# Block transposes of softmax weights through DMA: pieces of 4 KB instead of 1 KB, and twelve of sixteen DMAs on the sync engine

## The chip, the cores and the metric

The kernel runs on one core of a Trainium2 chip. A core has five engines that run their own instruction streams: TensorE (PE, with its weight loads listed apart as PEld), VectorE (DVE), ScalarE (ACT), GpSimd (POOL) and SyncE (SP). They meet through semaphores. DMAs are issued by an engine (here SP or POOL) into a queue and carried by 16 DMA engines. The metric is the device time of one execution in microseconds (us), the median over runs.

## The reference

Four transformer blocks act one after the other on x (4 batches, 1024 tokens, 256 channels), with a short context of 77 tokens for the cross-attention layers. All is float32. The change touches block L1, which has three attention layers with 4 heads of 64 channels: layer 0 attends to the context, layers 1 and 2 attend to the tokens themselves. Cut to what matters:

```python
def _mha_layer(q, k, v, Wq, bq, Wk, bk, Wv, bv, gamma, beta):
    Q = jax.nn.relu(q @ Wq + bq)          # likewise K, V; split into 4 heads of 64
    scores = jnp.einsum('hbqd,hbkd->hbqk', Qh, Kh) / jnp.sqrt(jnp.float32(dh))
    scores = jnp.where(key_mask[None, :, None, :] == 0.0, NEG, scores)
    attn = jax.nn.softmax(scores, axis=-1) * query_mask[None, :, :, None]
    out = jnp.einsum('hbqk,hbkd->hbqd', attn, Vh)
    return _layer_norm(out + q, gamma, beta)

q, k, v = (queries, keys, values)
for i in range(3):
    enc = _mha_layer(q, k, v, Wq[i], ...)
    enc = jax.nn.leaky_relu(enc @ Wff[i] + bff[i], negative_slope=0.2) + enc
    q, k, v = (enc, enc, enc)
```

## The kernel before

The program is laid out by a Python planner. Each (layer, batch) is an item. While an item attends, step by step ("units"), the planner weaves in the preparation of the next item (transposing x, projecting Q, K and V) and the end of the previous one (norm and feed-forward); each woven step has a cost, and `Pump` takes as many as the unit's share asks for. `Pipe.later(kind, delay, f)` puts off work to a later unit. The order on PE is the order in which the program is written. The order on the other engines is chosen by the compiler's scheduler, which also inserts all semaphores, and a buffer tag has a fixed number of slots that are reused in turn. DMAs issued by SP use eight completion semaphores in turn, those issued by POOL eight others.

A self layer of L1 (`Self4`) goes, per batch, over 2 pairs of heads p and 8 tiles t of 128 query tokens. One unit is one (p, t):

- `scores`: eight matmuls (L1262) give the scores of two heads, 128 queries by 1024 keys each, in two PSUM tiles `ss`. DVE takes the maximum of each row (L1273), ACT writes exp(score - max) into the SBUF tile `PR` and the row sums beside it (L1279).
- `turned_by_blocks`, one unit later: the weights must be transposed, since the next matmul contracts over the keys. DVE transposes every 32x32 block in place (L1291). For that to be enough on the DVE side, ACT has written the keys in the order (c, k, i) rather than (k, c, i), where a key's number is 128 k + 32 c + i. After every second tile t, sixteen DMAs (L1298) carry the blocks to the partitions where they belong: the DMA (c, a) reads partitions 32a to 32a+31 of `PR` and writes partitions 32c to 32c+31 of `PT`. It moves 128 KB: on each of 32 partitions four pieces (2 tiles by 2 heads) of 256 numbers, 1 KB each. a = 0 and 2 are issued by SP, a = 1 and 3 by POOL. Two tiles t, with their sixteen DMAs, are called a pair; there are 64 pairs in layers 1 and 2.
- `weighted`: two units and three units after the pair's second transposes are issued, 16 matmuls each (L1334) multiply V by `PT`, then ACT copies the sums (L1512) and, after four tiles, `normal` divides by the row sums and adds to x.

`PR` (tag "E") and `PT` (tag "B") have two slots of 16 KB per partition each. So the exp of a pair waits for the sixteen DMAs of the pair two before it, and the DMAs of a pair wait for the L1334 matmuls of the pair two before it.

Other users of the two DMA-issuing engines in this stage: SP loads the weights of the next layer (L1028, L1033), moves the mask row `nrow` (L1179), which the matmul L1231 reads, and `thirds` (a bias row cut into three bfloat16 rows by DVE, L2060 to L2063, each moved by a small DMA, L2061), which L1187 and L1402 read. POOL computes powers for the norms (L1385, between DVE's L1383 and L1387).

The flag `net.blocks` is true in the branch that runs here, taken when the mask leaves only a few keys to attend to in the network's first self-attention; the other branch (`turned`) transposes on PE and does not run.

Of the kernel before, what the change touches and what calls it, by code (L numbers as in the profile page):

```python
# [17 lines left out]
P = 128  # L18
NB, S, C, SC = 4, 1024, 256, 77
NT = S // P  # L20
# [102 lines left out]
class Pipe:  # L123
# [15 lines left out]
    def unit(self, scores=None, cost=0.0):  # L139
        self.call("full")  # L140
        if scores:
            scores()
        self.call("next")
        self.now += cost
        self.pump()
        for kind in ("turn", "late", "col"):
            self.call(kind)
        self.u += 1

    def run(self, items):  # L150
        pump = Pump(self, 1, items[0].start(), [])
        pump.until(lambda: items[0].halves >= 1)
        left = pump.lists[0]
        before = None
        for a, b in zip(items, items[1:]):
            b.prev = a
        for i, item in enumerate(items):
            last = i + 1 == len(items)
            first = left + ([] if last else items[i + 1].start())
            second = (before.end() if before else []) + (item.end() if last else [])  # L160
            left = []
            idle = item.idle()
            self.pump = pump = Pump(self, item.units + idle, item.more() + first, second)
            for _ in range(idle):
                self.unit()
            for scores in item.attend():
                self.unit(scores, item.cost)
            assert last or not any(pump.lists)
            before = item
        while self.due:  # L170
            pump.n = 0
            self.unit()
        pump.n = pump.units - 1
        pump()
# [33 lines left out]
class Cross16(Item):  # L208
# [147 lines left out]
    def scores(self, g, c):  # L356

        net, h = self.net, H16
        nc = net.nc
        e, s = g // 2, g % 2  # L360
        if g % 2 == 0:
            self.pts = net.tile("B", [SC, 2, h.J, 512], name="PT")
        pt = self.pts[:, g % 2]
        pbs = [net.pb.tile([P, 2, 512], F32, tag="pb", name="pb") for _ in range(2)]
        for j in range(h.J):
            rows = slice(32 * j, 32 * j + 32)
            nc.tensor.matmul(  # L367
                pbs[j // 2][:SC, j % 2, :], self.ka[rows, e, 2 * (j % 2) + s, :], self.qt[rows, e, ts(c, 512)],
                start=True, stop=False,
            )  # L370
        for j in range(h.J):
            rows = slice(32 * j, 32 * j + 3 * G)
            nc.tensor.matmul(  # L373
                pbs[j // 2][:SC, j % 2, :], net.pick16[rows, g, :], self.sh[rows, c, :], start=False, stop=True
            )
        for i in range(2):
            nc.scalar.activation(pt[:, 2 * i : 2 * i + 2, :], pbs[i][:SC], AF.Exp, scale=self.l.scale)  # L377
        net.pipe.later("col", 0, lambda: self.weighted(g, c, pt))

    def weighted(self, g, c, pt):  # L380
        net, l, h = self.net, self.l, H16
        nc = net.nc
        po = net.p1.tile([P, 512], F32, tag="p1", name="po")
        for j in range(h.J):
            col = self.head(g, j) * h.vs
            nc.tensor.matmul(  # L386
                po[ts(j, h.slot), :], l.v[:, self.b, col : col + h.vw], pt[:, j, :], start=True, stop=True
            )
        ot = net.tile("OT", [P, 512], name="OT")
        net.evac(ot, po)  # L390
        net.pipe.later("late", 1, lambda: self.normal(g, c, ot))
# [249 lines left out]
class Layer16Self:  # L641


    scale, norm, eps, out, ff, has_wo = 0.25, 1, None, None, None, True
# [168 lines left out]
class LayerFew:  # L813
# [3 lines left out]
    scale, norm, eps, out, ff, has_wo = 0.25, 1, None, None, None, True  # L817
# [303 lines left out]
class Self4(Item):  # L1121
# [133 lines left out]
    def scores(self, p, t):  # L1255
        net = self.net
        nc = net.nc
        ss = [net.pb.tile([P, 2, 512], F32, tag="pb", name="ss") for _ in range(2)]
        for k in range(2):
            for h in range(2):  # L1260
                rows = slice(64 * h, 64 * h + 64)
                nc.tensor.matmul(  # L1262
                    ss[h][:, k, :], self.qk[p][rows, 0, ts(t, P)], self.qk[p][rows, 1, ts(k, 512)],
                    start=True, stop=True,
                )
        if not net.blocks:
            pr = net.tile("E", [P, 2, S], name="PR")
        elif t % 2 == 0:
            self.pr = net.tile("E", [P, 2, 2, S], name="PR")
        for h in range(2):  # L1270
            at = slice(2 * p + h, 2 * p + h + 1)
            s2 = ss[h].rearrange("p k n -> p (k n)")
            nc.vector.tensor_reduce(self.nm[:, t, at], s2, AX.X, ALU.max, negate=True)  # L1273
            if net.blocks:
                out = self.pr[:, t % 2, h, :].rearrange("p (c k i) -> p k c i", c=4, i=32)
                s2 = s2.rearrange("p (k c i) -> p k c i", c=4, i=32)
            else:
                out = pr[:, h, :]
            nc.scalar.activation(out, s2, AF.Exp, bias=self.nm[:, t, at], accum_out=self.sums[:, t, at])  # L1279
        if net.blocks:  # L1280
            net.pipe.later("next", 1, lambda pr=self.pr: self.turned_by_blocks(p, t, pr))
        else:
            net.pipe.later("full", 1, lambda: self.turned(p, t, pr))

    def turned_by_blocks(self, p, t, pr):


        net = self.net
        nc = net.nc
        part = pr[:, t % 2].rearrange("p h s -> p (h s)")  # L1290
        nc.vector.transpose(part, part)  # L1291
        if t % 2 == 0:
            return

        pt = net.tile("B", [P, 2, 2, 4, NT, 32], name="PT")
        for c in range(4):
            for a in range(4):
                (nc.sync, nc.gpsimd)[a % 2].dma_start(  # L1298
                    out=pt[ts(c, 32), :, :, a].rearrange("p t h k j -> p (t h) (k j)"),
                    in_=pr[ts(a, 32), :, :, ts(c, 256)].rearrange("p t h n -> p (t h) n"),  # L1300
                )
        state = []
        for half in range(2):
            net.pipe.later("turn", 2 + half, lambda half=half: self.weighted(p, t, pt, half, state))
# [19 lines left out]
    def weighted(self, p, t, pts, half, state):  # L1324
        net = self.net
        nc = net.nc
        if half == 0:
            state.append(net.p1.tile([P, 2, P], F32, tag="p1", name="po"))
        po = state[0]
        if net.blocks:  # L1330
            po = po.rearrange("p t (a j) -> p t a j", a=4)
        for k in range(4 * half, 4 * half + 4):
            for h in range(2):
                nc.tensor.matmul(  # L1334
                    po[64 * h : 64 * h + 64], self.v[:, k, 64 * (2 * p + h) : 64 * (2 * p + h) + 64],
                    pts[:, :, h, :, k, :] if net.blocks else pts[:, :, h, k, :], start=k == 0, stop=k == NT - 1,
                )
        if half:
            if t % 4 == 1:
                self.ot = net.tile("OT", [P, 4, P], name="OT")  # L1340
            at = t % 4 - 1
            net.carry(self.ot[:, at : at + 2, :], state[0])
            if at:
                net.pipe.later("late", 1, lambda ot=self.ot: self.normal(p, t - 3, ot))
# [853 lines left out]
```

## Time and profile before

| | us |
|---|---|
| median of 3 runs | 2396.89 |
| lowest, highest run | 2395.11, 2406.44 |
| the profiled execution | 2396.79 |
| its span, first to last instruction | 2394.9 |
| exp L1279, 256 times, mean of one | 1.114 |
| DVE transpose L1291, 128 times, mean of one | 2.311 |
| row maximum L1273, 256 times, mean of one | 1.210 |
| scores L1262, 1024 matmuls, busy in all | 324.8 |
| weighted L1334, 2048 matmuls, busy in all | 251.1 |
| POOL issues of L1298, 512, busy in all | 279.6 |

The page gives busy time per engine and 40 equal slices of the span (59.9 us each); each digit is the busy share of a slice in tenths. The slices show where the block DMAs run:

```profile
PE   6899999999898979999999899999999899999996
...
DVE  6665553534424565888888788888888656656765
...
DMA  5000010000000000667776577766787400000000
GB/s 147 1 3 14 5 36 1 1 3 5 12 1 7 1 5 1 146 147 152 151 156 144 123 151 157 151 142 141 148 163 143 97 5 1 5 1 1 27 18 28
```

The sixteen slices with DMA at 4 or more after the first one are layers 1 and 2 of L1. "Idle before" in the groups of instructions is time in which an engine stood still ahead of an instruction, with the instruction whose semaphore ended it; idle time of an engine that nothing waits for costs nothing.

### The profile page before, as it was taken

Reading aid. Unit: us, or ns where it says so; the run is one execution under the profiler, and the core shown is the slowest. Engines: PE = TensorE matmul, PEld = TensorE weight load, DVE = VectorE, ACT = ScalarE, POOL = GpSimd, SP = SyncE. Lnnn points to the kernel's source line nnn. Section 1 sums busy time; section 2 is a strip of 40 time slices with the busy share of each in tenths; the row PEclk is TensorE's granted clock in tenths of the full one; section 3 lists DMA queues with packets and bytes.
Section 4 is the critical chain, followed back from the end, with each engine's and each line's share of the span. In section 5 each row is a group of like instructions: output and inputs, shape, how many; then the busy total and the mean of one; then the engine's idle time right before and its main releaser. Section 6 shows DMA issues by size and latency. Waiting matters only on the chain. (4 is left out here: it accounts for less than half of the span.)

```text
span 2394.9 us, 31195 instructions
## 1 busy us (share of the span) xinstructions
PE 2204.3 (92%) x11035; PEld 1204.8 (50%) x11035; DVE 1582.6 (66%) x3167; ACT 930.2 (39%) x1828; POOL 380.4 (16%) x648
## 2 busy tenths in 40 slices
PE   6899999999898979999999899999999899999996
PEld 3565446566577655545454445454545344444442
DVE  6665553534424565888888788888888656656765
ACT  2222332222232355545454454444444234434333
POOL 2000000000000000333333233333333100000000
PEclk8999989989998998999999999999999899999988
DMA  5000010000000000667776577766787400000000
GB/s 147 1 3 14 5 36 1 1 3 5 12 1 7 1 5 1 146 147 152 151 156 144 123 151 157 151 142 141 148 163 143 97 5 1 5 1 1 27 18 28
DMA packets 148677, 158.01 MB, mean 66 GB/s; under 512 B 51432, under 2 KB 130849, under 8 KB 148513
## 3 DMA queue, kind: packets, MB, share of 16 engines
q1 hardware_dynamic: 122161, 85.63, 17.2%
q0 software_dynamic: 25296, 69.24, 13.1%
q8 instruction: 91, 1.49, 0.3%
q10 hardware_dynamic: 1056, 1.05, 0.1%
q14 instruction: 73, 0.60, 0.1%
HBM read 17.41 MB, written 4.19 MB: 9 GB/s over the span
## 5 line engine op out<-in xcount | busy, mean ns | idle before, releaser
L1279 ACT ACTIVATE PR<-ss,nm 128x1024 f32<-128x1024 f32 x256 | 284.7, 1114 | 366.2 <-DVE nm L1273 290.2
L1291 DVE STREAM_TRANSPOSE PR<-PR 128x2048 f32<-128x2048 f32 x128 | 295.8, 2311 | 128.9 <-ACT PR L1279 114.3
L1298 POOL DMA_DIRECT2D PT<-PR x512 | 279.6, 554 | 577.7 <-PE ss L1262 236.7
L1262 PE MATMUL ss<-QK 64*128 64x512 f32 x1024 | 324.8, 628 | 28.8 <-ACT PR L1279 28.5
L1273 DVE TENSOR_REDUCE nm<-ss 128x1 f32<-128x1024 f32 x256 | 299.6, 1210 | 13.8 <-PE ss L1262 13.8
L377 ACT ACTIVATE PT<-pb 77x1024 f32<-77x1024 f32 x192 | 185.4, 1015 | 193.2 <-PE pb L373 193.2
L1334 PE MATMUL po<-PT,V 128*64 128x256 f32 x2048 | 251.1, 387 | 5.1 <-DMA PT<-PR 5.1
L281 DVE TENSOR_REDUCE mx<-pa 128x4 f32<-128x308 f32 x384 | 161.4, 470 | 83.7 <-PE pa L276 82.5
L1262 PEld LDWEIGHTS ss<-QK 64*128 64x128 f32 x1024 | 113.3, 187 | 176.8 <-ACT PR L1279 99.7
L1334 PEld LDWEIGHTS po<-PT,V 128*64 128x64 f32 x2048 | 136.6, 137 | 108.4 <-issue 51.1
L276 PE MATMUL pa<-KA,QT 64*128 64x308 f32 x768 | 169.1, 486 | 14.0 <-DVE mx L281 12.8
L1545 POOL TENSOR_TENSOR pw<-va,minus_half 128x4 f32<-128x4 f32 (+1 forms) x28 | 38.8, 1384 | 714.5 <-DVE va L1543 542.0
L386 PE MATMUL po<-PT,Vc 77*32 77x512 f32 x768 | 140.4, 639 | 7.6 <-ACT PT L377 7.0
L276 PEld LDWEIGHTS pa<-KA,QT 64*128 64x128 f32 x768 | 84.3, 193 | 99.1 <-issue 37.0
L604 PE MATMUL pp<-hF,w 128*128 128x256 f32 x512 | 116.9, 382 | 0.0
L367 PE MATMUL pb<-QT,KA 32*77 32x512 f32 x768 | 114.1, 665 | 0.0
L619 PE MATMUL pp<-w,hid 128*128 128x256 f32 x512 | 113.7, 379 | 0.0
L619 PEld LDWEIGHTS pp<-w,hid 128*128 128x128 f32 x512 | 97.0, 190 | 16.5 <-issue 2.2
L604 PEld LDWEIGHTS pp<-hF,w 128*128 128x128 f32 x512 | 95.6, 190 | 18.2 <-issue 6.0
L266 PE MATMUL pp<-hT,wq 128*128 128x512 f32 x192 | 98.0, 646 | 5.5 <-ACT hT L1507 5.0
L1536 DVE BATCH_NORM_STATS2 st<-x 128x6 f32<-128x256 f32 x256 | 97.7, 403 | 3.2 <-DMA x<-in_x 2.3
L1405 PE MATMUL pp<-wo,hE 128*128 128x256 f32 x384 | 96.4, 393 | 1.6 <-ACT hE L1512 1.6
(256 smaller groups left out, 3079.5 us busy)
## 6 DMA issues: line engine op xcount, KB each, us to landing
PT<-PR SPq DMA_DIRECT2D x512, 128.0 KB
PT<-PR POOLq DMA_DIRECT2D x512, 128.0 KB, 4.9
x<-in_x SPq DMA_DIRECT2D x4, 1024.0 KB
out<-x SPq DMA_DIRECT2D x8, 512.0 KB
w<-in_ff_w SPq DMA_DIRECT2D x2, 1024.0 KB
gb<-in_norms POOLq DMA_DIRECT2D x5, 256.0 KB, 6.6
wk<-in_l_wk SPq DMA_DIRECT2D x10, 128.0 KB
wv<-in_l_wv SPq DMA_DIRECT2D x5, 256.0 KB
```

The costliest lines, as they stand in the source:

```text
L276: nc.tensor.matmul(pas[i], self.qt[rows, e, ts(t, P)], self.ka[rows, e, :, :], start=True, stop=True)
L281: nc.vector.tensor_reduce(out, pas[i].rearrange("p (j s) k -> p j s k", s=2), AX.X, ALU.max, negate=True)
L377: nc.scalar.activation(pt[:, 2 * i : 2 * i + 2, :], pbs[i][:SC], AF.Exp, scale=self.l.scale)
L386: nc.tensor.matmul(po[ts(j, h.slot), :], l.v[:, self.b, col : col + h.vw], pt[:, j, :], start=True, stop=True)
L604: nc.tensor.matmul(pp[:, i, :], self.w1[:, cc, ts(f + i, P)], s["hT"][:, cc, ts(q, 2 * P)], start=cc == 0, stop=cc == NC - 1)
L619: nc.tensor.matmul(pp[:, u, :], s["a"][:, f, ts(u, P)], self.w2[:, f, :], start=f == 0, stop=f == NF - 1)
L1262: nc.tensor.matmul(ss[h][:, k, :], self.qk[p][rows, 0, ts(t, P)], self.qk[p][rows, 1, ts(k, 512)], start=True, stop=True,)
L1273: nc.vector.tensor_reduce(self.nm[:, t, at], s2, AX.X, ALU.max, negate=True)
L1279: nc.scalar.activation(out, s2, AF.Exp, bias=self.nm[:, t, at], accum_out=self.sums[:, t, at])
L1291: nc.vector.transpose(part, part)
L1298: (nc.sync, nc.gpsimd)[a % 2].dma_start(out=pt[ts(c, 32), :, :, a].rearrange("p t h k j -> p (t h) (k j)"), in_=pr[ts(a, 32), :, :, ts(c, ...
L1334: nc.tensor.matmul(po[64 * h : 64 * h + 64], self.v[:, k, 64 * (2 * p + h) : 64 * (2 * p + h) + 64], pts[:, :, h, :, k, :] if net.blocks e ...
```

## The change

The tile `PR` gets the key block c as its outermost index, [P, 4 (c), 2 (t), 2 (h), 256], so that what one DMA reads from a partition is one run of 1024 numbers, 4 KB. `PT` gets the source block a outermost, [P, 4 (a), 2 (t), 2 (h), NT, 32], so that what one DMA writes to a partition is one run too. The exp now writes runs of 32 at a larger stride, the DVE transpose works on four runs of 512 instead of one of 2048, and the matmul L1334 reads the same 2 x 4 x 32 columns at other strides. Of the sixteen DMAs of a pair, SP issues those with a = 0, 1 and 2 (twelve instead of eight), POOL those with a = 3 (four instead of eight). Nothing else differs; the numbers computed are the same.

```diff
         elif t % 2 == 0:
-            self.pr = net.tile("E", [P, 2, 2, S], name="PR")
+            self.pr = net.tile("E", [P, 4, 2, 2, S // 4], name="PR")
...
             if net.blocks:
-                out = self.pr[:, t % 2, h, :].rearrange("p (c k i) -> p k c i", c=4, i=32)
+                out = self.pr[:, :, t % 2, h, :].rearrange("p c (k i) -> p k c i", i=32)
                 s2 = s2.rearrange("p (k c i) -> p k c i", c=4, i=32)
...
-        part = pr[:, t % 2].rearrange("p h s -> p (h s)")
+        part = pr[:, :, t % 2].rearrange("p c h n -> p c (h n)")
         nc.vector.transpose(part, part)
         if t % 2 == 0:
             return
 
-        pt = net.tile("B", [P, 2, 2, 4, NT, 32], name="PT")
+        pt = net.tile("B", [P, 4, 2, 2, NT, 32], name="PT")
         for c in range(4):
             for a in range(4):
-                (nc.sync, nc.gpsimd)[a % 2].dma_start(
-                    out=pt[ts(c, 32), :, :, a].rearrange("p t h k j -> p (t h) (k j)"),
-                    in_=pr[ts(a, 32), :, :, ts(c, 256)].rearrange("p t h n -> p (t h) n"),
+                (nc.gpsimd if a == 3 else nc.sync).dma_start(
+                    out=pt[ts(c, 32), a].rearrange("p t h k j -> p (t h k j)"),
+                    in_=pr[ts(a, 32), c].rearrange("p t h n -> p (t h n)"),
                 )
...
-                    pts[:, :, h, :, k, :] if net.blocks else pts[:, :, h, k, :], start=k == 0, stop=k == NT - 1,
+                    pts[:, :, :, h, k, :].rearrange("p a t j -> p t a j") if net.blocks else pts[:, :, h, k, :], start=k == 0, stop=k == NT - 1,
```

## The prediction

> **What bounds the kernel now.** I read the page first, then the stage in which the changed lines run, then who waits there, then the two DMA queues.
>
> ```profile
> span 2394.9 us, 31195 instructions
> PE 2204.3 (92%) x11035; PEld 1204.8 (50%) x11035; DVE 1582.6 (66%) x3167; ACT 930.2 (39%) x1828; POOL 380.4 (16%) x648
> ...
> q1 hardware_dynamic: 122161, 85.63, 17.2%
> q0 software_dynamic: 25296, 69.24, 13.1%
> ```
>
> The L1 self layers run from about 950 to 1900 us; only there do the DMA engines work for long. Eight steady pairs in the middle of it, as busy time by engine (span, PE, PEld, DVE, ACT, POOL, granted clock, DMA share, GB/s):
>
> ```profile
> 1430.00:1546.00 116.00, 111.30 (x547) 55.18 (x547) 98.15 (x129) 56.95 (x120) 37.96 (x68) 1.00 0.71 150
> ```
>
> A pair (two token tiles, one set of sixteen block DMAs) takes 116.4/8 = 14.55 us from one second transpose to that of eight pairs later. PE is busy 96% of it and DVE 85%; the DMA engines are 71% busy and have room. Over 960 to 1900 us PE stands idle 52.9 us of 940. The list of waits says for whom:
>
> ```profile
> PE ss L1262 <- ACT PR L1279: 28.5, 38, 2.1
> ...
> PE pv L1187 <- DMA thirds<-third: 6.9, 1, 6.9
> ...
> PE po L1334 <- DMA PT<-PR: 5.1, 1, 5.1
> ```
>
> Columns: total us, times, longest. Among 64 pairs PE waited once for the block DMAs, in the last pair. ACT and DVE show 27.2 us (8 times) and 14.4 us (16 times) "DMA PT<-PR" before L1279 and L1291; those I believe only in part, because the semaphores named are shared by eight DMAs in turn and rise for the next pair's DMAs too. In the one case that I followed (exp at 994.69) the DMAs of the slot's earlier user had landed some 3 us before, and the maximum it needs had just ended.
>
> The issue rows, and the tightest undisturbed pair of the stage:
>
> ```profile
> L1298 SPq DMA_DIRECT2D PT<-PR x512: 585/806/1982, 965.3 to 1894.0; - x171
> L1298 POOL DMA_DIRECT2D PT<-PR x512: 550/552/620, 965.5 to 1890.6; - x171
> ```
> ```profile
> 1307.61 7.96 SPq L1298 DMA_DIRECT2D PT<-PR  x8
> ...
> 1308.13 4.41 POOL L1298 DMA_DIRECT2D PT<-PR  x8 [1.67 <-DVE rs L1388]
> ...
> 1320.33 1.95 PE L1334 MATMUL po<-PT,V 128*64 128x256 f32 x16
> ...
> 1321.90 1.11 ACT L1279 ACTIVATE PR<-ss,nm 128x1024 f32<-128x1024 f32 x1 [3.17 <-DVE nm L1273]
> ```
>
> The first two are ns min/median/max of one issue; the others are start, length, engine, line. Eight SP issues take 8 us; the data of this burst ended 11.4 us after the transpose (packet records). Its first reader, L1334, came 12.8 us after the transpose and the next writer of that PR slot 14.4 us after. In most pairs these two come 15 to 18 us after, with the last landing at about 12.1 us. So the DMAs have 1 us of slack in the worst pair and 3 to 6 in the others.
>
> **Part by part.**
>
> SP issues. Removed: 8 per pair of four 1 KB pieces per partition; added: 12 of one 4 KB piece. In the records of steady bursts the first three SP issues take 0.59 us each and the fourth to seventh 1.1, 1.1, 1.4 and 1.3 us (means); the fourth waits until about the first has landed (2.5 us after the transpose), so some queue is full after three or four. Bounds: 0.37 us (SP's store out<-x, 372 ns) to 1.23 us (mean of those four). I take 0.60: a DMA leaves 2 pieces on each DMA engine instead of 8, so a queue that counts pieces does not fill. Then 12 x 0.60 = 7.2 us instead of 8.0. High end: 12 x 1.23 = 14.8 us.
>
> POOL issues: 8 x 0.55 = 4.4 us become 4 x 0.55 = 2.2 us. POOL also runs the power L1385, which DVE's L1387 awaits; it gains at most 2.2 us at two places per batch, on DVE work that has other work around it. I take 0.
>
> Data. Same 2.1 MB per pair. In the packet records a 1 KB piece of the SP queue takes 79.4 ns, a 4 KB packet of the POOL queue 290 ns; four 1 KB pieces are 318. A block DMA (128 KB on 16 engines) is 8 x 79.4 = 0.635 us of data by the first, 2 x 290 = 0.58 by the second. The sixteen: 9.7 us before ((8 x 0.635) + (8 x 0.58)), 9.3 us after. Bounds for the SP piece: 186 ns (4 KB pieces of w<-in_ff_w, from HBM, alone) to 318. With the first landing at 2.5 us the last comes at 2.5 + 15 x 0.58 = 11.2 us; at 0.635, at 12.0. Today it is 12.1. So a burst lands 0 to 1 us earlier, in front of 3 to 6 us of slack: 0 on the path. If that cover were gone (a reader 3 us earlier), it would be 0.9 us x 64 = 58 us.
>
> A rule of the Trainium skill speaks against the larger piece. The row is 318 against 290 ns, 9%. The page "DMA: Bandwidth & Descriptors", section "Why small descriptors are slow (HBM only)", says that SBUF to SBUF transfers don't suffer the penalty of small pieces, and prices the one they have at about 3 cycles per packet of 32-byte beats; an estimate from it for 1 KB against 4 KB is (32+3) x 4 = 140 against 131 cycles, 6%. By its sentence the data phase would stay 9.7 us, by its figure 9.4; both vanish in the slack.
>
> Queue order. SP's own waits: a DMA waits for the last DMA on its semaphore, and SP uses eight in turn. The ninth to twelfth issue of a burst now wait for the first to fourth of the same burst, which today land 2.5, 5.1, 5.7 and 7.9 us after the transpose; they would issue at 4.8 to 6.6 us. At worst about 1 us at the end of the burst, inside the slack. What stands behind bursts on SP: nrow L1179 (issued up to 7 us after its row is made, read by L1231 20 us or more after the issue), the weight loads (tens of us early), and the thirds L2061. Only the thirds have PE behind them: around 1334 to 1340 us PE lost 6.9 us, with two PT issues (1.27 us) between two thirds. One more issue there is 0.6 to 1.2 us: +1, once; if the order falls better, -1. I take 0.
>
> Waits that engines check. Each pair's DMAs use 8 + 8 semaphores; PE, DVE and ACT each run eight or nine semaphore instructions, about 0.1 us apart, before L1334, L1291 and L1279. Afterwards 8 + 4, so two fewer: 0.2 us per engine and pair. They run while the engine is busy, except before DVE's L1291 in 16 places. 16 x 0.2 = 3 us of DVE time, little of it on the path: -0.5.
>
> Last pair. Its SP issues wait for the PT slot until 1886.5, the data land at 1897.7, PE waits 5.1 us until 1898.7. A burst 0.9 us shorter is -1 us; range 0 to -2.
>
> Compute layout. Transpose L1291 keeps 2048 elements, now as 4 runs of 512; bounds 2.31 us and 4 x 0.69 (L1411, 128x512) = 2.76; I take 2.31, since it is the same instruction. At 2.76 DVE would spend 0.9 us more per pair out of 2.2 idle. The exp L1279 already scatters runs of 32 and costs 1114 ns, as the plain L995 of the same size does (1114). L1334 reads runs of 32 in 387 ns, plain columns of 256 take 392 (L1405). Larger strides: 0.
>
> Sum: 0 + 0 + 0 - 0.5 - 1 = -1.5 us. The profiled execution was 2396.79 us (span 2394.9 and 1.9 around it), within 0.1 of the median 2396.89. Prediction 2395; own range of this case 2388 to 2402 (thirds and last pair both ways, slack lost in the tight pairs).
>
> **Rivals.** Bound of "faster" or "slower": 0.5%, 12 us, about what a measurement can tell here (the three runs spread by 11).
>
> Faster: the DMA waits of ACT and DVE are real. For: 27.2 + 14.4 us are listed, and PE's largest wait is for that ACT line. Against: the slack computed above, and DVE's maximum ending at the same moment. With PE's 5.1 and 6.9 all would be 54 us; half of it gives 2370.
>
> Slower: SP's queue becomes the bound. Twelve of sixteen DMAs pass one queue; if it counts DMAs, not pieces, each of the twelve costs 1.23 us. Then 14.8 + about 0.5 of waits exceed the 14.55 us of a pair: 0.7 x 60 = 42 us, and 2.6 once (landing at 14.8 + 4.7 = 19.5 us against a reader at 16.9): 2442. It decides from (14.55 - 0.5)/12 = 1.17 us per issue. For: the fourth issue stalls at three outstanding DMAs. Against: POOL's share of the engines ends after some 6 us, and alone the queue drains one DMA per 0.6 us. If the pieces were cut to 1 KB again, so that the change does not do what it says, an issue stays at 0.95 us, 11.4 us a burst, with landings near 16: the same place, perhaps +10.
>
> Slower by order: SP, DVE and ACT are ordered by a planner, whose order moves when DMAs change queue. The two restless stretches (1300 to 1360, PE idle 8.6 us; 1780 to 1900, 15.7 us) could double: 2421.
>
> **How the numbers follow.** Hidden 0.60, faster 0.18, SP bound 0.12, order 0.10. A little of the hidden case lies over either bound, which changes nothing after rounding. Faster 0.19, same 0.58, slower 0.23. Range 2372 to 2430: it takes in half of the faster case, the reordered one and a mild SP bound, and leaves out about 0.07 below and 0.1 above.
>
> **What would show it.** Right: SP issues near 0.6 us without the rise from the fourth on, a burst in 7 to 8 us, last landing at 11 to 12 us, pairs still 14.5 us apart, PE's 28.5 us before L1262 unchanged, L1291 at 2.31 us. Wrong: SP issues above 1.17 us and PE waiting for "DMA PT<-PR" in many pairs (SP bound); pairs shorter than 14.3 us with the DMA waits of ACT gone (faster); L1291 above 2.5 us; new PE idle time at the ends of layers (order).

## The result and the profile after

The changed kernel takes 2460.19 us in the median of 4 runs (2456.11 to 2467.91), the kernel before, run beside it, 2401.66 (2395.11 to 2411.99). The ratio is 1.0252, with a 95% interval of 1.0218 to 1.0285: 2.5% slower, where 2395 us were forecast with a range up to 2430.

The page of the changed kernel: span and busy time by engine, the two queues, and four of the costliest groups.

```profile
span 2461.6 us, 30806 instructions
PE 2264.8 (92%) x11035; PEld 1225.7 (50%) x11035; DVE 1586.9 (64%) x3167; ACT 929.6 (38%) x1828; POOL 227.6 (9%) x392
...
q1 hardware_dynamic: 85297, 119.20, 19.5%
q0 software_dynamic: 13008, 35.67, 5.8%
...
L1291 DVE STREAM_TRANSPOSE PR<-PR 128x2048 f32<-128x2048 f32 x128 | 295.6, 2309 | 171.4 <-ACT PR L1279 133.9
L1262 PE MATMUL ss<-QK 64*128 64x512 f32 x1024 | 358.7, 647 | 32.1 <-ACT PR L1279 31.0
L1279 ACT ACTIVATE PR<-ss,nm 128x1024 f32<-128x1024 f32 x256 | 283.9, 1113 | 272.9 <-DVE nm L1273 263.0
L1273 DVE TENSOR_REDUCE nm<-ss 128x1 f32<-128x1024 f32 x256 | 300.4, 1209 | 12.2 <-PE ss L1262 12.1
```

The same work was done at the same price: the exp takes 1113 ns (1114 before), the transpose 2309 (2311), the maximum 1209 (1210); DVE and ACT are busy for as long as before. The packets of the SP queue fell from 122161 to 85297, and their share of the engines' time rose only from 17.2% to 19.5% with 39% more bytes. One group grew: the scores L1262 are "busy" for 358.7 us instead of 324.8, with the same number of matmuls.

The issue rows (ns min/median/max of one issue) hold no trouble either:

```profile
L1298 SPq DMA_DIRECT2D PT<-PR x768: 507/591/2102, 965.2 to 1953.7; - x192
L1298 POOL DMA_DIRECT2D PT<-PR x256: 489/489/580, 965.5 to 1946.8; - x128
```

Nor does PE wait for the block DMAs, but for once, in the last pair, as before. PE's waits from 950 to 2000 us (total us, times, longest):

```profile
PE ss L1262 <- ACT PR L1279: 31.0, 27, 2.9
PE pt L1167 <- ACT hT L1512: 15.2, 5, 3.1
PE pv L1187 <- DMA thirds<-third: 7.1, 1, 7.1
PE po L1334 <- DMA wv<-in_l_wv: 5.0, 1, 5.0
```

The last line is, as I read it, that one wait, from 1952.1 to 1957.1 us: the last burst was issued on SP from 1945.13 to 1954.29, its data ended at 1955.8, and the load that the list names was issued right behind it.

Where the time went shows in busy time by stretch, the self layers of the kernel before and then of the changed one (columns as in the prediction; the two stretches begin and end at the same work):

```profile
950.00:1900.00 950.00, 897.14 (x4364) 442.53 (x4364) 788.99 (x1022) 445.04 (x906) 300.59 (x536) 0.98 0.70 146
```
```profile
950.00:1958.00 1008.00, 944.27 (x4363) 460.04 (x4363) 792.38 (x1022) 445.07 (x906) 147.93 (x280) 0.96 0.55 137
```

The stage is 58 us longer, and PE's idle time in it rose only from 52.9 us (950 - 897.1) to 63.7 (1008 - 944.3). The other 47 us are counted as busy PE, though the median of one L1262 is 589 ns in both; its mean went from 628 to 647. The granted clock and the starts of the matmuls show what they are.

The trace lists stretches in which PE is granted half its clock. The self layers have 6 of them before (33 us in all) and 17 after (87 us). Of PE's busy time, 29 us lie in them before and 79 us after; outside them it is 868 and 866 us. One L1262 takes 1057 ns there in the median, and 589 outside. The changed kernel once more: a pause of PE and the sixteen L1334 behind it (start, length), then the busy time of L1334 alone in that half-clock stretch and in one at full clock (span, PE, PEld, granted clock, DMA share, GB/s):

```profile
1475.34 1.12 PE L1167 MATMUL pt<-ident,x 128*128 128x128 f32 x4 [3.08 <-ACT hT L1512]
1476.38 3.68 PE L1334 MATMUL po<-PT,V 128*64 128x256 f32 x16
```
```profile
1474.70:1481.40 6.70, 3.68 (x16) 1.72 (x16) 0.50 0.03 7
1484.00:1490.70 6.70, 1.95 (x16) 1.06 (x16) 1.00 0.94 211
```

Each of the 23 stretches begins some 1.5 to 4.5 us after PE has begun a pause of 1.3 us or more. Of the pauses of 2 us or more, 3 of 3 before and 16 of 17 after were followed by one; of 15 pauses between 1.3 and 2 us in the two kernels, 4 were. So the changed kernel has hardly more idle time, but its pauses are longer, and work at half clock comes with them.

The rest of the "busy" time is PE waiting inside the scores. When both score tiles are free, the matmuls of the two heads start 6 or 7 ns apart and the eight of a unit take 1.99 us; otherwise they take up to 3.7 us, most often 3.1. At full clock 57 of 123 units take more than 2.4 us before, and 87 of 114 after. In all of these 144 the exp of the preceding unit's second head was still running when the eight began; in 86 of the 93 others it had ended.

Compared step by step, from the start of one matmul to that of the next, the 58 us are: 27 in steps that touch a half-clock stretch, 25 in steps between score matmuls at full clock, 6 in pauses at full clock. This is one execution of each kernel; over the whole span the changed kernel was granted 0.940 to 0.947 of the clock in its four runs, the kernel before 0.945 to 0.964 in the runs beside the experiments.

PE runs the same matmuls in the same order in both kernels, so each can be compared with itself. How many us later than in the kernel before the same matmul starts, against its time there:

```
time before   950  1000  1100  1200  1300  1400  1500  1600  1700  1800  1900  2100
later by      0.0   1.7  10.0  16.9  24.6  32.2  39.0  49.1  49.9  54.2  58.4  58.2
```

The loss is no single stall. It builds up all along the stage that has block DMAs, by some 6 us in 100. Before it there is none; behind it, from 2100 us to the end, another 11 came in this execution, of which layout_only (below), whose time is that of the kernel before, shows 8.

What does differ is ACT. Its waits in the changed kernel, 950 to 2000 us:

```profile
ACT PR L1279 <- DVE nm L1273: 263.0, 68, 5.7
ACT V L1194 <- PE pv L1190: 56.4, 14, 6.3
ACT QK L1233 <- PE pp L1226: 43.8, 22, 3.5
ACT QK L1233 <- PE pp L1231: 42.8, 15, 4.0
...
ACT low L1410 <- PE pp L1405: 30.9, 12, 3.8
```

In the kernel before:

```profile
ACT low L1410 <- PE pp L1405: 10.6, 6, 2.6
ACT V L1194 <- PE pv L1190: 9.7, 3, 6.9
ACT QK L1233 <- PE pp L1231: 3.9, 2, 3.7
```

ACT now stands for 174 us before evictions (its copies of PE's results out of PSUM) of projected work (V, QK, low) whose matmuls PE has not done, 24 before. What lies behind such an eviction in ACT's queue? The timeline of the changed kernel, one unit (start, length, engine, line; in brackets the idle time before and what ended it), the maxima first and then ACT:

```profile
1482.72 2.36 DVE L1273 TENSOR_REDUCE nm<-ss 128x1 f32<-128x1024 f32 x2 [1.20 <-PE ss L1262]
```
```profile
1480.40 0.21 ACT L1355 ACTIVATE e<-nm 128x8 f32<-128x8 f32 x1
1485.30 0.84 ACT L1194 ACTIVATE V<-pv,f 128x256 f32<-128x256 f32 x2 [4.68 <-PE pv L1190]
1486.02 1.12 ACT L1279 ACTIVATE PR<-ss,nm 128x1024 f32<-128x1024 f32 x1
```

And an eviction of V in the kernel before:

```profile
1447.48 1.11 ACT L1279 ACTIVATE PR<-ss,nm 128x1024 f32<-128x1024 f32 x1 [2.70 <-DVE nm L1273]
...
1448.58 1.11 ACT L1279 ACTIVATE PR<-ss,nm 128x1024 f32<-128x1024 f32 x1
...
1449.67 0.84 ACT L1194 ACTIVATE V<-pv,f 128x256 f32<-128x256 f32 x2
```

After the change the first of the two maxima is done near 1483.9, ACT is idle, and the exp starts at 1486.02, since the eviction of V stands ahead of it and waits for PE. Before, the exps came first, at once after their maximum, and V behind them. Two PSUM tiles hold scores, one for each head of a unit, and the exp frees its tile for the next unit's scores, so PE soon waits for a late exp, in the two ways shown above. From the records of all 256 exps: an exp starts 0.13 us after its maximum ends before the change (34 us in all), 0.89 us after it (227 us).

The order on ACT, DVE, POOL and SP is the scheduler's. The instruction lists of the two built kernels show that it chose another one: 252 of ACT's 1370 places and 479 of DVE's 3104 hold another instruction; PE's order, which is written, is the same in both.

### The profile page after: what moved, and what is told of

It reads as the page before. It is cut to its first block, busy times and chain, and to the rows that moved or that the text cites. A ratio compares the mean times of both kernels' runs of the same rounds, so it can differ in the third digit from the quotient of the medians.

```text
span 2461.6 us, 30806 instructions
## 1 busy us (share of the span) xinstructions
PE 2264.8 (92%) x11035; PEld 1225.7 (50%) x11035; DVE 1586.9 (64%) x3167; ACT 929.6 (38%) x1828; POOL 227.6 (9%) x392
## 3 DMA queue, kind: packets, MB, share of 16 engines
q1 hardware_dynamic: 85297, 119.20, 19.5%
## 5 line engine op out<-in xcount | busy, mean ns | idle before, releaser
L1291 DVE STREAM_TRANSPOSE PR<-PR 128x2048 f32<-128x2048 f32 x128 | 295.6, 2309 | 171.4 <-ACT PR L1279 133.9
L1262 PE MATMUL ss<-QK 64*128 64x512 f32 x1024 | 358.7, 647 | 32.1 <-ACT PR L1279 31.0
L1279 ACT ACTIVATE PR<-ss,nm 128x1024 f32<-128x1024 f32 x256 | 283.9, 1113 | 272.9 <-DVE nm L1273 263.0
L1273 DVE TENSOR_REDUCE nm<-ss 128x1 f32<-128x1024 f32 x256 | 300.4, 1209 | 12.2 <-PE ss L1262 12.1
L1334 PE MATMUL po<-PT,V 128*64 128x256 f32 x2048 | 261.1, 399 | 5.0 <-DMA wv<-in_l_wv 5.0
L1262 PEld LDWEIGHTS ss<-QK 64*128 64x128 f32 x1024 | 125.2, 192 | 200.6 <-ACT PR L1279 119.9
L1298 POOL DMA_DIRECT2D PT<-PR x256 | 124.8, 494 | 815.1 <-DVE r L1359 132.7
L1334 PEld LDWEIGHTS po<-PT,V 128*64 128x64 f32 x2048 | 140.7, 141 | 115.9 <-issue 61.0
L367 PE MATMUL pb<-QT,KA 32*77 32x512 f32 x768 | 119.4, 695 | 0.0
```

The source lines that it names most:

```text
L1262: nc.tensor.matmul(ss[h][:, k, :], self.qk[p][rows, 0, ts(t, P)], self.qk[p][rows, 1, ts(k, 512)], start=True, stop=True,)
L1298: (nc.gpsimd if a == 3 else nc.sync).dma_start(out=pt[ts(c, 32), a].rearrange("p t h k j -> p (t h k j)"), in_=pr[ts(a, 32), c].rearrange( ...
L1334: nc.tensor.matmul(po[64 * h : 64 * h + 64], self.v[:, k, 64 * (2 * p + h) : 64 * (2 * p + h) + 64], pts[:, :, :, h, k, :].rearrange("p a ...
```

## The experiments

Two theories were open at first. **Order**: the new order of ACT and DVE is the loss, and neither pieces nor queues cost anything themselves. **Cost**: the new layout, or twelve DMAs on SP's queue, cost the time by themselves.

**One part of the change at a time, and orders exchanged.** layout_only is the changed kernel with the old choice of issuers, split_only the kernel before with the new one:

```diff
-                (nc.gpsimd if a == 3 else nc.sync).dma_start(
+                (nc.sync, nc.gpsimd)[a % 2].dma_start(
```
```diff
-                (nc.sync, nc.gpsimd)[a % 2].dma_start(
+                (nc.gpsimd if a == 3 else nc.sync).dma_start(
```

after_old_order and before_new_order hold ACT and DVE to the other kernel's instruction order, by dependencies without a semaphore between neighbours; `ORDERS` holds that order as a list of instruction numbers:

```diff
                 self.rest(first(), out)
+                if self.blocks:
+                    keep_order(self.tc, self.nc)
...
+def keep_order(tc, nc):
+    made = {i.name: i for i in nc.cur_bb.bb.instructions}
+    how = mybir.DependencyInfo(mybir.DependencyClass.NoSync, mybir.DependencyReason.DATA)
+    for text in ORDERS.values():
+        names = [n for n in kept_order(text) if n in made]
+        for a, b in zip(names, names[1:]):
+            tc.add_manual_dep(made[b], a, how, reason="kept order")
```

> The new layout of PR and PT (one 4 KB piece per partition and DMA) with the old issuers (a even on SP, a odd on POOL). The instructions of ACT, DVE, POOL and SP stand in the same order as before the change. Order theory (the time comes from the order that the compiler's scheduler gave ACT and DVE): no change, 2388 to 2402 us. Piece theory (4 KB pieces, the larger strides of exp, transpose or matmul cost time on the chip): about 2460. Queue theory (twelve DMAs on SP cost): no change either.

> The old layout (four 1 KB pieces per partition and DMA) with the new issuers (twelve of sixteen on SP). ACT and DVE stand in the same order as after the change. Order theory: all of the loss, 2450 to 2475 us. Piece theory: no loss, about 2397. Queue theory: the loss, and more of it than in the changed kernel, since 1 KB pieces fill SP's queue sooner: 2460 to 2520.

> The changed kernel whole, with its twelve SP issues and 4 KB pieces, but ACT and DVE are held to the order in which their instructions stood before the change (edges of issue order only, no waits). POOL and SP keep nearly the order of the changed kernel. Order theory: back to 2385 to 2402 us. Queue and piece theories: stays at 2450 to 2470.

> The kernel before, with its eight and eight issues and 1 KB pieces, but ACT and DVE are held to the order in which their instructions stand in the changed kernel. Order theory: 2450 to 2475 us although no DMA is changed. Queue and piece theories: 2397.

Measured, beside 2399.11 for the kernel before: layout_only 2398.19, ratio 0.9991 (0.9962 to 1.0019); split_only 2454.35, 1.0232 (1.0147 to 1.0317); after_old_order 2415.29, 1.0044 (1.0007 to 1.0082); before_new_order 2499.73, 1.0426 (1.0343 to 1.0509).

The layout is worth nothing, though it cut the DMA share of the stage from 0.70 to 0.64. The choice of issuers is the whole loss, and it is what changes the order: layout_only has the order of the kernel before on every engine, split_only that of the changed kernel. Given the old order, the changed kernel loses 45 of its 61 us (2460 - 2415, 2460 - 2399); given the new order, the kernel before, with its own DMAs, loses 101. The order is the cause. The expectation for after_old_order, 2385 to 2402, was missed by 13 us, and that for before_new_order, 2450 to 2475, by 25. That the new order costs the kernel before more than the changed one shows that an order does not have a price of its own: it is good or bad for the other queues that it meets.

**Which engine, and which instructions.** Counted in the instruction lists, as pairs of an exp and an eviction (V, QK, low) that is written after it and stands ahead of it on ACT: 9 in the kernel before, 179 in the changed one. old_act gives ACT the order of the kernel before and keeps DVE and POOL as in the changed kernel. exp_first ties nothing on ACT but those evictions, and keeps DVE, POOL and SP in the changed kernel's order:

```diff
-            nc.scalar.activation(out, s2, AF.Exp, bias=self.nm[:, t, at], accum_out=self.sums[:, t, at])
+            net.exp = nc.scalar.activation(out, s2, AF.Exp, bias=self.nm[:, t, at], accum_out=self.sums[:, t, at])
...
-            nc.scalar.mul(low, pp, 0.2)
+            net.behind_exp(nc.scalar.mul(low, pp, 0.2))
...
+    def behind_exp(self, made):
+        """An eviction stays behind the exps that are written ahead of it."""
+        if self.blocks and self.exp is not None:
+            how = mybir.DependencyInfo(mybir.DependencyClass.NoSync, mybir.DependencyReason.DATA)
+            self.tc.add_manual_dep(made.ins, self.exp.ins.name, how, reason="behind exp")
```

with the same wrapper around the evictions of V (L1194) and QK (L1233). exp_first_old_dve has the rule and DVE in the order of the kernel before; before_exp_first has the rule alone, in the kernel before.

> The changed kernel, with ScalarE held to the instruction order of the kernel before and VectorE and GpSimd exactly in the order of the changed kernel. It splits the reordering by engine: with both engines in the old order the changed kernel took 2415, with both in the new order 2460. If ScalarE's order is the cause (evictions of QK, V and low that wait for TensorE stand ahead of exps whose maximum is ready): 2400 to 2425, exps starting on average less than 0.25 us after their maximum (0.89 in the changed kernel, 0.13 before). If VectorE's order is (its maxima come late behind other work): 2440 to 2465. If both count: 2425 to 2440.

> The changed kernel, in which every eviction of V, QK and low on ScalarE is kept behind the exps that are written ahead of it; VectorE, GpSimd and SyncE keep the changed kernel's order exactly. In the instruction lists, 79 QK, 66 V and 34 low evictions stand ahead of exps that are written before them in the changed kernel, 8, 0 and 1 in the kernel before, and none here. If these places are the cause: 2395 to 2425, exps less than 0.25 us behind their maximum, scores no longer waiting more than in the kernel before. If it is some other part of ScalarE's order: 2430 to 2460, though exps start sooner. If VectorE's order is: 2440 to 2465.

> As exp_first, and VectorE held to the order of the kernel before as well. If ScalarE's evictions ahead of exps are the whole cause, VectorE's order is worth nothing: within 8 of exp_first. If VectorE's order is worth something of its own: 10 or more below exp_first. If the rest of 16 us that the changed kernel in the old order showed is a wait of the first weights of the next layer behind block DMAs on SyncE's queue, about 1310 to 1320 us, it is still here as one TensorE wait of 10 us or more, and the time is 2405 to 2420; if that wait came from the held order alone, it is gone and the time is 2392 to 2402.

> The kernel before, with the same rule (evictions of V, QK and low behind the exps written ahead of them). Only 9 such places exist in it, so by the theory of ScalarE's order it is worth 9 of the 179 places, 3 us: 2390 to 2400. If the rule itself costs (an eviction kept back holds a PSUM buffer that TensorE wants): 2410 or more. If VectorE's order is the cause: no difference, 2395 to 2402.

Measured, beside 2399.73: old_act 2423.46, ratio 1.0108 (1.0084 to 1.0132); exp_first 2422.14, 1.0124 (1.0077 to 1.0172); exp_first_old_dve 2410.02, 1.0035 (1.0004 to 1.0066); before_exp_first 2398.32, 0.9985 (0.9962 to 1.0007). The exps start 0.21, 0.20, 0.20 and 0.12 us after their maximum.

Three wrapped lines give back 38 us of the changed kernel's loss, as much as the whole old order of ACT does (37). The scheduler moved other ACT instructions in exp_first too, but not back: with the evictions left out, ACT's list differs from the changed kernel's in 56 places and from that of the kernel before in 70. One part of the expectation was missed: the scores still wait longer in all than in the kernel before (35.0 us against 28.5). In the kernel before, where the 9 pairs are worth 3 us at most, the rule changes nothing that can be told. Some 22 us are left in exp_first. There 28 maxima start late behind a transpose L1291 that stands ahead of them on DVE, by 58 us in all (2 of them, 3 us, in the kernel before). With DVE's old order 12 of the 22 us go. The four runs of exp_first spread from 2409 to 2441, so these 12 are weak by themselves; the same step from old_act to after_old_order is worth 8. A new stall comes with it; DVE in exp_first_old_dve:

```profile
1302.26 0.48 DVE L1594 SCALAR_TENSOR_TENSOR x<-x,rs,gb 128x256 f32<-128x256 f32 x1
1317.27 0.28 DVE L2070 CAST third<-rows 1x256 bf16<-1x256 f32 x1 [14.53 <-DMA rows<-in_rows]
1317.48 2.34 DVE L1273 TENSOR_REDUCE nm<-ss 128x1 f32<-128x1024 f32 x2
```

and SP's queue there (in this kernel the lines from L1512 on are numbered 8 or 10 higher):

```profile
1301.51 8.58 SPq L1298 DMA_DIRECT2D PT<-PR  x12
1310.18 1.32 SPq L1028 DMA_DIRECT2D wk<-in_l_wk  x2
1311.55 0.62 SPq L1033 DMA_DIRECT2D wv<-in_l_wv  x1
1312.23 1.21 SPq L1028 DMA_DIRECT2D wq<-in_l_wq  x2
1313.48 0.62 SPq L1033 DMA_DIRECT2D wo<-in_l_wo  x1
1314.15 0.33 SPq L1045 DMA_DIRECT2D rows<-in_rows  x1
```

A bias row of 1 KB for the next layer is queued on SP behind twelve block DMAs and six weight loads, 12.6 us. DVE in its old order reaches the cast of that row early and stands 14.5 us, with a maximum behind it; PE then stands 14.8 us before L1262. In the kernel before, the same row was issued at 1302.00, ahead of the burst. after_old_order has the same wait (14.6 us). Here the queue of twelve does cost something, but only to an order that was made for a queue of eight.

**The row taken off that queue, the two queues exchanged, and DVE's order by itself.** rows_first is exp_first_old_dve with

```diff
-            nc.sync.dma_start(out=rows, in_=t["rows"][ROW[name] : ROW[name] + 1, at : at + C])
+            nc.gpsimd.dma_start(out=rows, in_=t["rows"][ROW[name] : ROW[name] + 1, at : at + C])
```

pool_twelve is the changed kernel with `(nc.sync if a == 3 else nc.gpsimd)`, and before_new_dve is before_exp_first with DVE held to the changed kernel's order.

> As exp_first_old_dve (exps first on ScalarE, VectorE in the order of the kernel before), with one DMA per layer and half, rows, issued by GpSimd instead of SyncE. There SyncE issued the rows of the next layer at 1314.2, behind twelve block DMAs (8.6 us) and six weight loads (3.9 us), VectorE stood 14.5 us before the cast of the first third, and TensorE 14.8 us before the next scores; in the kernel before the rows were issued at 1302.0, ahead of the burst. If that queue is the rest of the loss: the wait of 14.5 us is gone and the time is 2390 to 2402, as the kernel before. If the rest is spread (transfers, clock, more work per pair): 2405 to 2415, wait or no wait.

> The changed kernel with the two queues exchanged: GpSimd issues twelve of the sixteen block DMAs and SyncE four. SyncE's queue is then shorter than in the kernel before (4 x 0.6 = 2.4 us a pair), and GpSimd's has 12 x 0.49 = 5.9 us. In its instruction lists 82 QK, 58 V and 32 low evictions stand ahead of exps written before them, 172 against 179 in the changed kernel. If the order of ScalarE and VectorE sets the time, whichever queue carries the twelve: 2440 to 2470. If twelve on SyncE's queue is what costs: 2395 to 2410.

> The kernel before with exps first on ScalarE, and VectorE held to the order of the changed kernel. Without the last part it took 2398. If VectorE's order costs of its own (a transpose, which waits for its exps, stands ahead of a maximum whose scores are ready): 2408 to 2425, with maxima late behind L1291 some 28 times, as in exp_first. If ScalarE's order is the whole of it: 2394 to 2402.

Measured, beside 2401.83: rows_first 2392.22, ratio 0.9967 (0.9936 to 0.9998); pool_twelve 2435.97, 1.0146 (1.0090 to 1.0201); before_new_dve 2468.01, 1.0251 (1.0196 to 1.0306).

rows_first: the wait for the row is gone, and with it the rest of the loss. It is the first version that is below both kernels, by 0.3% of the kernel before, with an interval that ends just under 1. From the first scores to the start of the last transpose it takes 922.7 us (before 928.3, changed 986.9, exp_first_old_dve 944.8).

pool_twelve came out at 2436, just under what the order was expected to give and far above the 2395 to 2410 of a costly SP queue. SP now issues 256 block DMAs instead of 768, and the loss in the stage is 47 us instead of 59; the exps start 0.82 us after their maximum, for the same reason (172 pairs). So twelve on SP's queue is not what costs: rows_first has twelve there and loses nothing, and with four there 34 us are still lost. Of the 12 us between the two stages, an estimate from the traces accounts for 10: 61 us at half clock in it against 82 in the changed kernel.

before_new_dve missed its expectation by far: 2.5% slower, where 2408 to 2425 was thought possible. The exps are prompt (0.08 us). But PE stands 63.8 us before L1262, where it stood 28.5 in the kernel before, and the stage has 120 us at half clock instead of 27. DVE's waits there, 950 to 2000 us:

```profile
DVE PR L1291 <- ACT PR L1279: 81.0, 66, 1.8
DVE low L1411 <- ACT low L1410: 40.7, 20, 4.5
DVE rs L1387 <- POOL pw L1385: 33.0, 17, 2.9
```

DVE's order was made for a POOL with four issues a pair; here POOL has eight (4.4 us) ahead of the power that L1387 awaits, 33.0 us in all where the changed kernel waits 4.6. Thirty maxima came late behind a transpose L1291 that stood ahead of them, 86 us in all. Which of the two costs how much no run separates. DVE's order can cost as much as ACT's, in a setting it was not made for; so the 8 to 12 us that it is worth in the changed kernel are no property of it alone.

**Without any held order.** rule_only has the rule and the row on POOL; DVE is left to the scheduler.

> The changed kernel with two written edits and no held order: evictions of V, QK and low behind the exps written ahead of them, and the rows DMA issued by GpSimd. VectorE is left to the scheduler, whose order differs from the kernel before in 510 places. rows_first, the same with VectorE in the order of the kernel before, took 2392. If the reordered evictions and the queue of rows are the whole loss: 2388 to 2404. If VectorE's order is worth the 10 to 30 that exp_first against rows_first suggests: 2404 to 2425.

Measured 2404.14 beside 2398.54, ratio 1.0018 (0.9987 to 1.0050): no difference from the kernel before that can be told. It fell on the border of the two expectations, and its interval overlaps that of rows_first, so what DVE's order is still worth there is open.

## Why the prediction was wrong

The steps that priced the change itself held, but for one size:

- The layout: the exp, the transpose and L1334 at new strides cost nothing (1113 and 2309 ns; the median L1334 is 379 ns in both). So did 4 KB pieces: less data time, hidden, as layout_only shows with 0.9991.
- SP issues: 0.60 us was taken and the median is 0.591. But a burst of twelve takes 8.7 us in the median, not 7.2: a rise is still there, from the fourth issue to the sixth. In the packet records its last data end 10.7 us after the transpose in the median (11.9 before), where 11.2 to 12.0 was worked out. The cover of 3 to 6 us held. Only the last pair makes PE wait, 5.0 us as against 5.1, so the -1 for it did not come.
- The rivals "faster" and "SP bound": the first falls with layout_only, whose DMAs are lighter and whose time is the same; the second with 0.591 against the 1.17 from which it decides, and with pool_twelve.

The step that failed is **"Slower by order"**: "The two restless stretches ... could double: 2421", with a chance of 0.10, and no term in the sum. The mechanism was the right one; its place and size were not. It was charged only where PE was already seen to idle, at the ends of layers. In place of 24 us at those ends the runs show some 58 us spread over the whole stage, and split_only has 55 of them with the old pieces. For a new order acts in every unit: 128 units, each with two exps that can be put behind an eviction that waits for PE. The changed kernel's exps lose 193 us more than before behind their maxima (227 - 34), of which the stage shows 58. And the price of a pause was taken to be the pause: that PE is granted half its clock after longer ones, 27 of the 58 us, stands in no term. A price from the profile of before was possible: ACT had 148 such evictions in these 128 units (60 QK, 56 V, 32 low), its exps were on time by 0.13 us only because these stood behind them, and with two score tiles PE has little that covers a late exp.

The sign that was named for it, "new PE idle time at the ends of layers", would have missed it: idle time rose by 11 us, and 47 came as busy records, at half clock or inside the scores.

What the order cost in the changed kernel, taken away one by one: evictions ahead of exps 38 us (2460 to 2422), DVE's order 12 more (2422 to 2410, near the noise), the row behind the burst 18 more (2410 to 2392). The last two are tied to each other, since the wait for the row comes only with DVE's old order. Why the scheduler places evictions otherwise when four DMAs of a pair change engine was not looked into.

## What to carry to other kernels

Where a scheduler orders the engines, moving a DMA to another engine can reorder engines that the edit does not name; compare the instruction order of the two builds before pricing the parts, and price a changed order over every unit of the stage, not over the places that already idle. An in-order engine that feeds the bound (here ACT's exps) should have its urgent work ahead of evictions that wait for the bound engine, written as a rule and not left to chance. Small loads that an engine waits for did harm on the queue behind the bursts: moving one of them to the other queue took exp_first_old_dve from 2410 to 2392. And look at the granted clock and at the longest pauses of the bound engine, not only at the sum of its idle time.

## What the runs showed of the hardware

- The rise of SP's issue time does not go with small pieces. With 8 + 8 DMAs the fourth to seventh issue of a burst took 1.20, 1.10, 1.41 and 1.34 us in the median with 1 KB pieces, and 0.95, 1.27, 1.33 and 1.19 with 4 KB (layout_only). With 12 + 4 of 4 KB the fourth to sixth took 0.77, 1.09 and 0.94, and the rest 0.59 again; with only four on SP (pool_twelve) the fourth took 0.59. POOL's issue went from 550 ns (1 KB) to 489 (4 KB).
- A 4 KB piece of the SP queue took less than four of 1 KB in the mean of the packet records, with the same split of the queues: 284 ns (layout_only) against 4 x 79.4 = 318 with 8 + 8, and 257 against 4 x 73.2 = 293 (split_only) with 12 + 4. That is 11 to 12% less data time, none of it seen in the kernel's time.
- A stall need not show as idle time of the bound engine: 47 of 58 us were busy PE. After 19 of 20 PE pauses of 2 us or more in the two stages, a stretch at half clock followed, in which the median L1262 took 1057 ns instead of 589.
